# Reordering norms, moments and four copies in a three-layer attention kernel on one core

## The chip, the cores and the metric

The kernel runs on one core of a Trainium2 chip, as one program. The metric is the device time of an execution in microseconds (us), and the numbers given are medians over runs. A core has five engines that work side by side and meet at semaphores: TensorE (PE; its weight loads are listed apart as PEld), VectorE (DVE), ScalarE (ACT), GpSimd (POOL) and SyncE (SP), which here only issues DMA transfers. Each engine takes its own instructions strictly in the order in which the kernel writes them.

## The reference

Inputs are `x` and `ctx`, each 32 x 256 x 256 in fp32 (batch, tokens, features), and weights.

```python
# layer 0: attention with 16 heads of 16 columns; the result of batch element 0 is added to all 32
q, k, v = heads(x @ Wq.T), heads(ctx @ Wk.T), heads(ctx @ Wv.T)
x = x + attention(q, k, v, 1 / sqrt(16))[0]
# layer 1
norm_X = layernorm(ctx, n1w, n1b)
norm_F = layernorm(x, n2w, n2b)
attended = softmax(norm_F @ norm_X.T / 16) @ norm_X
h = gelu(attended @ fc1_w.T + fc1_b)                   # 4 hidden values per token
cross = h @ fc2_w.T + fc2_b
norm_cross = layernorm(cross, n3w, n3b)
self_att = softmax(norm_cross @ norm_cross.T / 16) @ norm_cross
out = norm_F + gamma2 * (cross + gamma1 * self_att)
```

In layer 0 only batch element 0 has to be computed. In layer 1 all 32 elements go through two layer norms, a 256 x 256 cross attention, and a self attention. Since `cross` has 4 hidden values and a bias behind it, the self attention needs few columns for each token (5 or 6 of a slot of 32).

## The kernel before

Everything of `x` stays in SBUF in one tile `x_all`, 128 partitions x 32 elements x 2 halves of the tokens x 256. Four batch elements make a quad; there are 8 quads. `ctx` comes in by quads into tiles `cq`, of which four exist at once. The order of the work on each engine is written out by hand (`tc.manual_schedule()`): the order of the calls is the order of the instructions on each engine's queue, and nothing is moved later. The one thing that the order does not settle is when a buffer is free: PSUM tiles come from pools with two banks for each of the tags `tp` and `et` (`bank`), and with two each for `sm` and `s` (pool `ps1`), and a tile waits for the readers of the tile that had its bank before.

The stages in order:

**Head, to about 53 us.** Layer 0 for element 0. `project(j)` and `head_step(j, ...)`, j = 0 to 3, each take four heads. `head_queries` (L392, L412) makes scores `sq` and VectorE takes their maxima `m_all`; `head_maxima` turns the maxima (`pm`) and adds them to the queries (`qmT`); `head_keys` (L437, L438) makes the scores `sk` again with the maxima taken off, and ScalarE exponentiates them into `eT_h`; `head_values` and `head_weighted` multiply by the values and divide (`ph`, `rd_h`, `att`). The three lists given to `head_step` put other work behind each of these: statistics and norms of the first three quads of `ctx`, the constants of the later layers, and the first transposes of `ctx` (`turn_c`). `turn_values` and `project_values` make the values `v1` of layer 0, in a bank `pp_v`.

**Steps 0 to 31, to about 190 us.** `first_step(s)` does the cross attention of one batch element s in a software pipeline. On each engine the calls of a step stand in the order of the function's text:

- `add_attention` has GpSimd issue a DMA that adds `att` to a quad of `x` (L647).
- `cross_turned(s - 2)` transposes the exponentials (TensorE, `pt_e`), and ScalarE copies them to `eTq` (L697).
- `stats_c(s + 12)` and `stats_x` let VectorE take means and variances of later elements (L202).
- `moments_x`, `moments_c` and `moments_both` turn those statistics into a factor `rs` and a shift `nmr`, on GpSimd (L213 to L227, with the power -1/2 in L218). They do so for 2, 4, 8 or 16 columns at once, one column for each half of an element; `moments_both(q + 2)` takes all of quad q + 2 of `x` and of quad q + 3 of `ctx`, 16 columns, in steps 7, 11, 15, 19.
- `turn_x(s + 1)` transposes the next element of `x` (`pt_x`), and ScalarE scales it into `nfT` (L657).
- `norm_x(n)` applies factor and shift to element n of `x`: half 0 on GpSimd (L298), half 1 on ScalarE (L300). From step 8 on n = s + 4.
- `turn_c(s + 4)` transposes an element of `ctx` (`pt_c`, TensorE), and VectorE copies it to `nxT` (L311).
- `norm_c(s + 8)` applies factor and shift to an element of `ctx`, both halves on GpSimd (L291, two instructions). Step s + 4 transposes it.
- `zeroed` clears tiles of the third layer in steps 8 to 15, and `scale_skip` (L666) scales `x` for the output from step 25 on; both are on GpSimd.
- `values`, `values_turned`, `cross_values` and `cross_weighted` (`pf`, `pv`) do the products with the values for a quad, in the second, third and fourth step of one.
- `cross_scores(s)` makes the scores `sc` (L675, TensorE), then VectorE takes the negated maxima `nm` (L685) and ScalarE the exponentials `e` (L688).
- Behind the step, at s = 3, GpSimd takes the moments of the fourth quad of `ctx` (`moments_c(3)`).

From step 20 the dictionaries `between` and `beside` add parts of the self attention to the steps: `hide` and `activate` (hidden values, GELU), `third_a` to `third_d` (layer norm and factors of the slots, GpSimd and VectorE; L854, L874 to L879, in which L876 is again a power), `turn_u`, `early_scores`, `early_weights`.

**Tail, to the end.** The steps B to B + 3 let the pipeline run empty. A loop over j = 3 to 7 works on the self attention by pairs of elements: `turn_t`, `turn_v`, `turn_u` transpose slots (L907 is the copy of `turn`), `pair_products` (L392) makes scores and outputs `po`, `scores_max` takes maxima, `weights` exponentials, `output` (L1040) adds to `x_all` and SyncE sends the result out. For j = 3, `turn_v(0)` is VectorE's, behind the maxima of the first pair.

Of the kernel before, what the change touches and what calls it, by code (L numbers as in the profile page):

```python
# [22 lines left out]
QB = 4  # L23
# [4 lines left out]
def tile_xattn_seq(  # L28
# [33 lines left out]
    nc = tc.nc  # L62
    B = x.shape[0]
# [16 lines left out]
    def bank(tag, name):  # L80
        return ps.tile([P, NC, D], F32, tag=tag, name=name)
# [178 lines left out]
    def moments_x(q, lo, hi):  # L260
        rn = moments(flat(st_of[q][:, 1, lo:hi]), (hi - lo) * NC, f"x{q}_{lo}")
        for b in range(lo, hi):
            mx_of[q * QB + b] = *rn, (b - lo) * NC
# [23 lines left out]
    def norm_c(n):  # L287
        rs, nmr, i = mc_of.pop(n)
        for t in range(NC):
            row = cq_of[n // QB][:, n % QB, t, :]  # L290
            nc.gpsimd.tensor_scalar(  # L291
                row, row, rs[:, i + t, :], nmr[:, i + t, :], ALU.mult, ALU.add
            )

    def norm_x(n):
        rs, nmr, i = mx_of.pop(n)
        row = x_all[:, n, 0, :]
        nc.gpsimd.tensor_scalar(row, row, rs[:, i, :], nmr[:, i, :], ALU.mult, ALU.add)  # L298
        row = x_all[:, n, 1, :]
        nc.scalar.activation(  # L300
            row, row, AF.Identity, bias=nmr[:, i + 1, :], scale=rs[:, i + 1, :]
        )
# [4 lines left out]
    def turn_c(n, copy=nc.vector.tensor_copy):  # L307
        q, b = n // QB, n % QB
        if b == 0:
            nxT_of[q] = wk.tile([P, QB, NC, D], F32, tag="nxT", name=f"nxT_{q}", bufs=2)  # L310
        copy(nxT_of[q][:, b], turned(cq_of[q][:, b], "tp", f"c_{n}"))  # L311
# [56 lines left out]
        nc.scalar.copy(wvT, turned(w_nat["v"], "tp", "wv"))  # L368

    def project_values():  # L370
        pp = bank("et", "pp_v")
        for t in range(NC):
            for dc in range(NC):
                nc.tensor.matmul(
                    pp[:, t, :],
                    c0T[:, dc, t * P : (t + 1) * P],
                    wvT[:, dc, :],
                    start=(dc == 0),
                    stop=(dc == NC - 1),
                )  # L380
        for t in range(NC):
            nc.vector.tensor_copy(
                v1[:, t, :, 0:DK], pp[:, t, :].rearrange("p (h e) -> p h e", e=DK)
            )
# [199 lines left out]
    def head_step(j, behind_queries=(), behind_maxima=(), behind_keys=()):  # L584
# [32 lines left out]
        2,  # L617
        [(head_values, 1), (project, 3)],
        [(head_weighted, 1), (setup_outer,), *((norm_c, n) for n in range(QB, 2 * QB))],
        [(turn_c, 0), *((stats_c, n) for n in range(2 * QB, 3 * QB)), (moments_c, 2)],  # L620
    )
    head_step(
        3,
# [7 lines left out]
        [(turn_c, 4)],  # L631
    )
    head_values(3)
    turn_c(5)
    head_weighted(3)


# [124 lines left out]
    def first_step(s, between=()):  # L762
        q, b = s // QB, s % QB
        if b == 0 and 2 <= q and q + 4 < NQ:
            load_c(q + 4)
        if s in (2, 3):
            add_attention((s + 1) * QB, (s + 2) * QB)
        elif b == 0 and 0 < q < NQ - 4:
            add_attention((q + 4) * QB, (q + 5) * QB)
        if 0 <= s - 2 < B:  # L770
            cross_turned(s - 2)
        if s < QB:
            stats_c(s + 3 * QB)
        if 2 <= s < 2 * QB:
            for n in (2 * s, 2 * s + 1):
                stats_x(n)
            if s < QB:
                ends = first_moments(2 * s, 2 * s + 2)
        if QB <= s and s + 3 * QB < B:
            stats_c(s + 3 * QB)  # L780
        if s >= 2 * QB and s + 2 * QB < B:
            stats_x(s + 2 * QB)
        if s == QB + 1:
            moments_x(2, 0, QB)
        if b == QB - 1 and 3 <= q + 2 < NQ:
            if q + 3 < NQ:
                moments_both(q + 2)
            else:
                moments_x(q + 2, 0, QB)
        if QB < s < B - 1:  # L790
            turn_x(s + 1)
        for n in {5: (8,), 6: (9, 10), 7: (11,)}.get(s, (s + QB,) if s > 7 else ()):
            if n < B:
                norm_x(n)
        if s + QB < B and s >= QB:
            turn_c(s + QB)
        if s >= QB and s + 2 * QB < B:
            norm_c(s + 2 * QB)
        for n, at in enumerate(scaled_at):
            if s == at:  # L800
                scale_skip(n)
        if 2 * QB <= s < 2 * QB + len(zeroed):
            nc.gpsimd.memset(*zeroed[s - 2 * QB])
        if b == 2 and 1 < q < NQ:
            values_turned(q)
        if b == 1 and 1 < q < NQ:
            values(q)
        if b == 2 and 0 < q <= NQ:
            cross_values(q - 1)
        if b == 3 and 0 < q <= NQ:  # L810
            cross_weighted(q - 1)
        for f, *args in between:
            f(*args)
        if s < B:
            softmax = cross_scores(s)
            if s <= QB:
                turn_x(s + 1)
            if s == 0:
                add_first(3)
            softmax()  # L820
        if s in (2, 3):
            ends()
        if s == QB - 1:
            moments_c(3)


    n_flat = n_all.rearrange("p g t b c -> p (g t b) c")
# [228 lines left out]
    for j in range(3, NQ):  # L1056


        turn_t(j - 1)
        sc0, b0 = pair_bank("s0", f"sc0_{2 * j}")  # L1060
        sc1, b1 = pair_bank("s1", f"sc1_{2 * j - 3}")
        pair_products(by_queries(2 * j, b0), by_keys(2 * j - 3, b1))
        if j == 3:
            first_step(B + 3)
            hide(6, 8)
            activate(6)
            third_a(3)
        scores_max(2 * j, sc0)
        turn_v(j - 3, by_vector if j == 3 else nc.scalar.copy)
        weights(2 * j - 3, sc1)  # L1070
        if j + 1 < NQ:
            turn_u(j + 1)
        po = out_banks(2 * j - 6)
        sc0, b0 = pair_bank("s0", f"sc0_{2 * j + 1}")
        pair_products(to_output(2 * j - 6, po), by_queries(2 * j + 1, b0))
        if j < NQ - 1:
            output(2 * j - 6, po)
            scores_max(2 * j + 1, sc0)
        else:
            scores_max(2 * j + 1, sc0)  # L1080
            output(2 * j - 6, po)
        self_values(j - 2)
        if j == NQ - 1:
            break
        if j == 3:
            third_b(3)
        if j == 4:
            third_d(3)
        sc1, b1 = pair_bank("s1", f"sc1_{2 * j - 2}")
        po = out_banks(2 * j - 5)  # L1090
        pair_products(by_keys(2 * j - 2, b1), to_output(2 * j - 5, po))
        weights(2 * j - 2, sc1)
        pa = self_weighted(j - 2)
        output(2 * j - 5, po)
        divide(j - 2, pa)
        if j == 3:
            third_c(3)
        done = len(scaled_at) + max(3 * (j - 3), 4 * (j - 3) - 2)
        for n in range(done, min(done + (3 if j < 5 else 4), B)):
            scale_skip(n)  # L1100
# [94 lines left out]
```

## Time and profile before

| what | value |
|---|---|
| median of 3 runs | 253.17 us |
| lowest and highest of the runs | 253.0 and 260.94 us |
| the profiled execution, time | 252.99 us |
| its span, first to last instruction | 251.0 us |
| its mean granted TensorE clock | 0.986 of full speed |
| TensorE busy | 219.1 us (87% of the span) |
| GpSimd busy | 181.7 us (72%) |
| VectorE busy | 171.7 us (68%) |
| ScalarE busy | 138.8 us (55%) |
| read from HBM, written to it | 17.73 MB, 8.39 MB |

The profile is of one execution. A row of a timeline gives the start in the span (us), the length, the engine, the line of the kernel, the operation with what it writes and reads, and in brackets how long the engine stood idle before it and what ended that. "x2" says that two such instructions ran one after the other. The chain of waits is followed back from the last instruction: at each step to what released it, or to the instruction before it on its engine. A name such as `pt_c` stands for all tiles of that name.

### The profile page before, as it was taken

Reading aid. Unit: us, or ns where it says so; the run is one execution under the profiler, and the core shown is the slowest. Engines: PE = TensorE matmul, PEld = TensorE weight load, DVE = VectorE, ACT = ScalarE, POOL = GpSimd, SP = SyncE. Lnnn points to the kernel's source line nnn. Section 1 sums busy time; section 2 is a strip of 40 time slices with the busy share of each in tenths; the row PEclk is TensorE's granted clock in tenths of the full one; section 3 lists DMA queues with packets and bytes.
Section 4 is the critical chain, followed back from the end, with each engine's and each line's share of the span. In section 5 each row is a group of like instructions: output and inputs, shape, how many; then the busy total and the mean of one; then the engine's idle time right before and its main releaser. Section 6 shows DMA issues by size and latency. Waiting matters only on the chain.

```text
span 251.0 us, 4961 instructions
## 1 busy us (share of the span) xinstructions
PE 219.1 (87%) x1813; PEld 159.5 (64%) x1813; DVE 171.7 (68%) x411; ACT 138.8 (55%) x271; POOL 181.7 (72%) x284
## 2 busy tenths in 40 slices
PE   8978785778975999999999997899999699999970
PEld 6656453446763979788797885666666455665540
DVE  1587875599897576778676684663546487876482
ACT  2231443447864976858768948538534735554610
POOL 8007999784799998999859999984159619999200
PEclk9999999999999999999999999999999889999996
DMA  6869999499999565390000000000000023442467
GB/s 210 292 192 373 387 387 330 169 203 251 208 183 158 167 106 107 125 168 2 3 1 1 3 0 3 0 5 2 3 0 0 3 111 142 167 161 93 171 228 275
DMA packets 18054, 33.81 MB, mean 135 GB/s; under 512 B 1191, under 2 KB 2158, under 8 KB 18030
## 3 DMA queue, kind: packets, MB, share of 16 engines
q1 hardware_dynamic: 13518, 25.37, 28.3%
q0 software_dynamic: 3696, 7.34, 16.9%
q10 hardware_dynamic: 816, 0.79, 0.9%
q8 instruction: 14, 0.23, 0.4%
q14 instruction: 10, 0.08, 0.1%
HBM read 17.73 MB, written 8.39 MB: 104 GB/s over the span
## 4 chain that ended last, share of the span: by engine, by line
PE 61%; DVE 19%; POOL 12%; ACT 3%; issue 3%; DVEq 0%; POOLq 0%; ACTq 0%
PE sc L675 16%; PE sc L392 9%; PE pt_c L193 4%; PE pt_x L193 4%; DVE st L202 4%; PE pt_e L193 3%; PE po L392 3%; PE pv L318 3%; PE pu L318 2%; POOL r L876 2%; PE pp L357 2%; POOL rs_x L218 2%; DVE x_all L1040 2%; PE pf L318 2%; DVE m_all L412 2%
## 5 line engine op out<-in xcount | busy, mean ns | idle before, releaser
L675 PE MATMUL sc<-nxT,nfT 128*128 128x256 f32 x256 | 62.5, 387 | 1.6 <-ACT nfT L657 1.6
L675 PEld LDWEIGHTS sc<-nxT,nfT 128*128 128x128 f32 x256 | 45.7, 190 | 13.3 <-issue 4.9
L688 ACT ACTIVATE e<-sc,nm 128x256 f32<-128x256 f32 x64 | 26.7, 470 | 25.8 <-DVE nm L685 25.8
L685 DVE TENSOR_REDUCE nm<-sc 128x2 f32<-128x512 f32 x32 | 22.1, 689 | 27.3 <-PE sc L675 14.1
L666 POOL TENSOR_TENSOR x_all<-x_all,w_bc 128x512 f32<-128x512 f32 x32 | 39.6, 1280 | 0.0
L657 ACT ACTIVATE nfT<-pt_x,bq,wq 128x256 f32<-128x256 f32 x64 | 33.1, 578 | 3.1 <-PE pt_x L193 3.1
L311 DVE COPY nxT<-pt_c 128x512 f32<-128x512 f32 x27 | 18.3, 679 | 11.2 <-PE pt_c L193 11.2
L193 PE MATMUL pt_x<-ident,x_all 128*128 128x128 f32 x132 | 20.3, 276 | 4.2 <-POOL x_all L298 1.9
L202 DVE BATCH_NORM_STATS2 st<-x_all 128x6 f32<-128x256 f32 x64 | 23.2, 412 | 0.1
L193 PE MATMUL pt_e<-ident,e 128*128 128x128 f32 x128 | 19.8, 276 | 2.2 <-ACT e L688 2.1
L392 PE MATMUL po<-w_out,vt 32*128 32x256 f32 x128 | 18.6, 417 | 3.4 <-DVE vt L907 2.2
L193 PE MATMUL pt_c<-ident,cq 128*128 128x128 f32 x132 | 20.3, 276 | 1.3 <-DVE ut L900 0.8
L1040 DVE TENSOR_TENSOR x_all<-po,x_all 128x512 f32<-128x512 f32 x26 | 16.7, 684 | 6.5 <-PE po L392 5.4
L202 DVE BATCH_NORM_STATS2 st<-cq 128x6 f32<-128x256 f32 x56 | 20.2, 412 | 0.0
L193 PEld LDWEIGHTS pt_x<-ident,x_all 128*128 128x128 f32 x132 | 15.5, 142 | 6.8 <-POOL x_all L298 3.3
L392 PE MATMUL sc<-ut 32*128 32x256 f32 x128 | 19.7, 419 | 0.0
L697 ACT COPY eTq<-pt_e 128x512 f32<-128x512 f32 x32 | 18.6, 585 | 1.9 <-PE pt_e L193 1.8
L291 POOL TENSOR_SCALAR cq<-cq,rs_b,nmr_b 128x256 f32<-128x256 f32 x32 | 19.4, 682 | 0.0
L392 PE MATMUL sc<-tt,ut 32*128 32x256 f32 x128 | 19.4, 403 | 0.0
L193 PEld LDWEIGHTS pt_e<-ident,e 128*128 128x128 f32 x128 | 15.4, 141 | 6.1 <-ACT e L688 3.2
L291 POOL TENSOR_SCALAR cq<-cq,rs_c,nmr_c 128x256 f32<-128x256 f32 x32 | 17.9, 589 | 0.1
L193 PEld LDWEIGHTS pt_c<-ident,cq 128*128 128x128 f32 x132 | 15.0, 141 | 4.0 <-issue 1.4
(204 smaller groups left out, 442.9 us busy)
## 6 DMA issues: line engine op xcount, KB each, us to landing
out_dram<-x_all SPq DMA_DIRECT2D x16, 512.0 KB
cq<-in_ctx_dram SPq DMA_DIRECT2D x7, 1024.0 KB
x_all<-att POOLq DMA_DIRECT2D x7, 1024.0 KB, 9.7
x_all<-in_x_dram SPq DMA_DIRECT2D x6, 1024.0 KB
x_all<-in_x_dram SPq DMA_DIRECT2D x1, 1792.0 KB
cq<-in_ctx_dram SPq DMA_DIRECT2D x1, 768.0 KB
wq_nat<-in_L_xattn_Wq_dram ACTq DMA_DIRECT2D x1, 256.0 KB
x_all<-in_x_dram SPq DMA_DIRECT2D x1, 256.0 KB
```

Source lines behind the costliest of these rows:

```text
L193: nc.tensor.transpose(pt[:, dc, t * P : (t + 1) * P], src[:, t, dc * P : (dc + 1) * P], ident)
L202: nc.vector.bn_stats(st[:, t, :], src[:, t, :])
L291: nc.gpsimd.tensor_scalar(row, row, rs[:, i + t, :], nmr[:, i + t, :], ALU.mult, ALU.add)
L311: copy(nxT_of[q][:, b], turned(cq_of[q][:, b], "tp", f"c_{n}"))
L392: nc.tensor.matmul(dst[i][:, t, :], lhs[r : r + SL, t * P : (t + 1) * P], rhs[r : r + SL, :], start=True, stop=True,)
L657: nc.scalar.activation(nfT_of[n][:, dc, :], px[:, dc, :], AF.Identity, bias=bq[:, dc : dc + 1], scale=wq2[:, dc : dc + 1],)
L666: nc.gpsimd.tensor_mul(x_all[:, n], x_all[:, n], w2_bc.unsqueeze(1).to_broadcast([P, NC, D]))
L675: nc.tensor.matmul(sc[:, qt, :], nfT[:, dc, qt * P : (qt + 1) * P], nxT[:, dc, :], start=(dc == 0), stop=(dc == NC - 1),)
L685: nc.vector.tensor_reduce(nm, sc, AX.X, ALU.max, negate=True)
L688: nc.scalar.activation(e[:, qt, :], sc[:, qt, :], AF.Exp, bias=nm[:, qt : qt + 1])
L697: nc.scalar.copy(eT_of[q][:, b], turned(e_of.pop(n), "et", f"e_{n}"))
L1040: nc.vector.tensor_add(x_all[:, n], po[i], x_all[:, n])
```

## The change

Six things change. (1) The bank of `pp_v` is taken from the tag `tp` instead of `et`. (2) The copies of `turn_c(0)` and `turn_c(5)` in the head go from VectorE to ScalarE. (3) The moments of x's third quad (elements 8 to 11) are taken in two pairs, at the end of steps 4 and 5, instead of all four at the start of step 5; x's norms 8 to 11 move to the ends of steps 5, 6, 6 and 7, behind those steps' exponentials on ScalarE; and the moments of the fourth quad of `ctx` move from the end of step 3 to the end of step 6. (4) c's norms, which ran eight elements ahead of the scores and four steps ahead of their transposes (steps 4 to 23), run six elements ahead of the scores and two steps ahead of their transposes: c 12 at the end of step 6, and element s + 6 in step s for s = 7 to 25. (5) x's norms of the last quad come one step later (s = 25 to 28, element s + 3). (6) In the tail `turn_v(0)` moves ahead of the first pair's products. No operation is added but one more set of moments (two of 4 columns in place of one of 8), and none is taken away.

```diff
--- before.py
+++ after.py
@@ -368,7 +368,7 @@
         nc.scalar.copy(wvT, turned(w_nat["v"], "tp", "wv"))
 
     def project_values():
-        pp = bank("et", "pp_v")
+        pp = bank("tp", "pp_v")
         for t in range(NC):
             for dc in range(NC):
                 nc.tensor.matmul(
@@ -617,7 +617,11 @@
         2,
         [(head_values, 1), (project, 3)],
         [(head_weighted, 1), (setup_outer,), *((norm_c, n) for n in range(QB, 2 * QB))],
-        [(turn_c, 0), *((stats_c, n) for n in range(2 * QB, 3 * QB)), (moments_c, 2)],
+        [
+            (turn_c, 0, on_scalar),
+            *((stats_c, n) for n in range(2 * QB, 3 * QB)),
+            (moments_c, 2),
+        ],
     )
     head_step(
         3,
@@ -631,7 +635,7 @@
         [(turn_c, 4)],
     )
     head_values(3)
-    turn_c(5)
+    turn_c(5, on_scalar)
     head_weighted(3)
 
 
@@ -780,8 +784,6 @@
             stats_c(s + 3 * QB)
         if s >= 2 * QB and s + 2 * QB < B:
             stats_x(s + 2 * QB)
-        if s == QB + 1:
-            moments_x(2, 0, QB)
         if b == QB - 1 and 3 <= q + 2 < NQ:
             if q + 3 < NQ:
                 moments_both(q + 2)
@@ -789,13 +791,14 @@
                 moments_x(q + 2, 0, QB)
         if QB < s < B - 1:
             turn_x(s + 1)
-        for n in {5: (8,), 6: (9, 10), 7: (11,)}.get(s, (s + QB,) if s > 7 else ()):
-            if n < B:
-                norm_x(n)
+        if 2 * QB <= s < B - 2 * QB:
+            norm_x(s + QB)
+        elif B - 2 * QB < s <= B - QB:
+            norm_x(s + QB - 1)
         if s + QB < B and s >= QB:
             turn_c(s + QB)
-        if s >= QB and s + 2 * QB < B:
-            norm_c(s + 2 * QB)
+        if QB + 2 < s < B - QB - 2:
+            norm_c(s + QB + 2)
         for n, at in enumerate(scaled_at):
             if s == at:
                 scale_skip(n)
@@ -820,8 +823,18 @@
             softmax()
         if s in (2, 3):
             ends()
-        if s == QB - 1:
+        elif s == QB:
+            moments_x(2, 0, 2)
+        elif s == QB + 1:
+            norm_x(2 * QB)
+            moments_x(2, 2, QB)
+        elif s == QB + 2:
+            norm_x(2 * QB + 1)
             moments_c(3)
+            norm_x(2 * QB + 2)
+            norm_c(3 * QB)
+        elif s == QB + 3:
+            norm_x(2 * QB + 3)
 
 
     n_flat = n_all.rearrange("p g t b c -> p (g t b) c")
@@ -1057,6 +1070,8 @@
 
 
         turn_t(j - 1)
+        if j == 3:
+            turn_v(0, by_vector)
         sc0, b0 = pair_bank("s0", f"sc0_{2 * j}")
         sc1, b1 = pair_bank("s1", f"sc1_{2 * j - 3}")
         pair_products(by_queries(2 * j, b0), by_keys(2 * j - 3, b1))
@@ -1066,7 +1081,8 @@
             activate(6)
             third_a(3)
         scores_max(2 * j, sc0)
-        turn_v(j - 3, by_vector if j == 3 else nc.scalar.copy)
+        if j > 3:
+            turn_v(j - 3)
         weights(2 * j - 3, sc1)
         if j + 1 < NQ:
             turn_u(j + 1)
```

## The prediction

> **What bounds the kernel now.** I read the page first, then the chain of waits in order of time, then timelines where that chain leaves TensorE.
>
> ```profile
> PE 219.1 (87%) x1813; PEld 159.5 (64%) x1813; DVE 171.7 (68%) x411; ACT 138.8 (55%) x271; POOL 181.7 (72%) x284
> ```
>
> TensorE is busy 87% of the span, so time is lost where it waits. GpSimd (POOL, 72%) is next. The chain in order of time (start, us, what):
>
> ```profile
> 70.73 1.65 POOL rs_c L218
> 72.87 1.34 POOL x_all L647
> 74.21 1.15 POOL cq L291 x2
> 76.49 1.66 POOL rs_x L218
> 80.38 1.08 POOL x_all L298 x2
> 81.48 0.63 PE pt_x L193 x4
> ...
> 97.74 1.73 PE sc L675 x8
> ...
> 103.39 0.44 PE pt_c L193 x4
> ```
>
> From 60 to 81 us the chain is mostly GpSimd's moments and norms; from 81 to 141 us it is TensorE. The scores of steps 4 to 13 start at 66.78, 71.90, 76.03, 82.60, 85.80, 89.84, 94.29, 97.74, 100.78 and 104.82. Where TensorE waits for nothing a step takes 3.04 (11 to 12), with pt_v 3.45 (10 to 11), with pv and pt_f 4.45 (9 to 10). Step 6 to 7 takes 6.57 and should take 3.45. ScalarE's timeline there says why:
>
> ```profile
> 78.66 0.60 ACT L300 ACTIVATE x_all<-x_all,nmr_x,rs_x 128x256 f32<-128x256 f32 x1 [4.86 <-POOL nmr_x L227]
> ```
>
> ScalarE stands 4.86 us at its half of x's norm 8; the exponentials of step 5 are queued behind it, and TensorE waits for them. The next views are GpSimd's at step 11, then all engines around step 25:
>
> ```profile
> 98.40 0.23 POOL L213 TENSOR_TENSOR df_b<-st 128x16 f32<-128x16 f32 x1 [0.98 <-DVE st L202]
> 99.69 2.93 POOL L218 TENSOR_TENSOR rs_b<-ve_b,neg_half 128x16 f32<-128x16 f32 x1
> 103.10 0.56 POOL L298 TENSOR_SCALAR x_all<-x_all,rs_b,nmr_b 128x256 f32<-128x256 f32 x1
> 103.64 1.09 POOL L291 TENSOR_SCALAR cq<-cq,rs_b,nmr_b 128x256 f32<-128x256 f32 x2
> ```
>
> ```profile
> 148.30 0.60 PE L193 MATMUL pt_c<-ident,cq 128*128 128x128 f32 x4
> 151.72 0.60 ACT L300 ACTIVATE x_all<-x_all,nmr_x,rs_x 128x256 f32<-128x256 f32 x1 [4.11 <-POOL nmr_x L227]
> 152.22 1.10 POOL L291 TENSOR_SCALAR cq<-cq,rs_b,nmr_b 128x256 f32<-128x256 f32 x2
> 199.41 0.86 PE L392 MATMUL po<-w_out,vt 32*128 32x256 f32 x2 [2.21 <-DVE vt L907]
> ```
>
> Once in four steps a block of moments over 16 columns holds GpSimd from 98.40 to 103.10, and the norms of that step come behind it. That costs nothing now: c's norm in that place is needed four steps later.
>
> **Part 1, ScalarE copies keys 0 and 5.** VectorE's rows in order:
>
> ```profile
> 33.74 0.69 DVE L311 COPY nxT<-pt_c 128x512 f32<-128x512 f32 x1 [1.27 <-PE pt_c L193]
> 34.35 2.70 DVE L202 BATCH_NORM_STATS2 st<-cq 128x6 f32<-128x256 f32 x8
> 36.97 2.40 DVE L412 TENSOR_REDUCE m_all<-sq 128x4 f32<-128x1024 f32 x3
> ```
>
> Without the copy the statistics start at 32.46 (end of mkT) and end at 35.2. The maxima then wait only for their scores (34.34 + 1.15), so they start at 35.5 and not at 36.97: 1.5 earlier, and pm, qmT, sk, eT_h, ph and att follow one another from there. Key 5's copy (46.49 to 47.18) stood before rd_h, whose input was there at 46.80: 0.2. ScalarE has room: 35.20 to 36.55 and 46.31 to 48.00 are free, a copy takes 0.59. GpSimd bounds the gain: its norms of c's third quad end at 46.99 and the DMA issue behind them takes 0.9, so rs_x cannot start before 47.9 (before: 49.90), at most 2.0 earlier. I take -1.6; bounds 0 and -2.0. If ScalarE had no room, the copy would push eT_h by its 0.59.
>
> **Part 2, pp_v in the other bank.** The last ten sq matmuls waited for the copies of v until 18.48 and may go 0.4 earlier. VectorE is busy without a gap from 17.58 to 22.07, which hides it: 0, bounds -0.4 and 0.
>
> **Part 3, order on GpSimd, steps 4 to 9,** on the clock of before. Norms of x 6 and 7 end at 69.54. DMA issue 0.89 (72.86 to 73.75): 70.43. Moments of 4 columns: 1.19 of small operations, pow 1.03, two products 0.50, so 2.72: 73.15. x 8 (0.55): 73.70. Second pair (its statistics end at 72.84): 76.42; x 9: 76.97. c's moments (69.54 to 72.86, 3.32): 80.29; x 10: 80.84; c 12 (1.08): 81.92; moments of 16 columns (4.7): 86.6; c 13: 87.7; x 11, DMA, x 12, c 14: 90.7. ScalarE's half of x 8 now stands behind the exponentials, so step 7's scores start at 76.03 + 3.45 = 79.5, 3.1 earlier; step 8's at 82.5 (x 9 and c 12 are in time, c 12 by 0.2). Step 9 wants c 13 at 82.5 + 1.73 + 0.87 = 85.1 and gets it at 87.7: TensorE waits 2.5 (its first transpose needs only half of c 13), and its scores start at 87.7 + 0.4 + 1.0 = 89.1 instead of 89.84. Net -0.75; bounds -3.1 (c 13 in time) and +0.5 (GpSimd's rows 1.2 longer). SP's load of c 6 waits for step 7's transposes only, so it comes earlier and delays nobody.
>
> **Part 4, c's norms two steps ahead.** From step 11 on, step s norms c s+6, which step s+2 transposes. The instruction order of the built program shows the 16-column moments of steps 11, 15 and 19 straight ahead of c 17, 21 and 25. In the fence above that place ends at 104.73, while TensorE wants c 17 at 103.39: 1.34 late, 1.2 after the first transpose. The same two rows are 119.73 against 118.37 and 134.69 against 133.36. The moments start when VectorE's statistics are done, and those follow the scores of the step before, so a stall moves both alike and the next quad pays again: 3 x 1.2 = +3.7; bounds 0 and +4.1. Behind the waiting transposes stand pf and sc, hence the whole step.
>
> **Part 5, steps 23 to 26.** x's last norms one step later take ScalarE's 4.11 us wait off the exponentials of step 24. But c 29 now sits where c 31 sat, behind pow of r (2.92), w_k and x's last moments: 152.22 to 153.3, with two of VectorE's rows out of its way 153.05, and TensorE wants it at 148.30. It stands 4.7, step 25's scores start at 154.4 instead of 149.83. Then sc 1.9, VectorE's nm and ut (1.4, they free pt_c's bank), pt_c, pt_f and pv (1.66): step 26 at 159.4 instead of 156.80, so +2.7; bounds -1.9 (c 29 in time) and +3.1. c 30 and c 31 follow in time.
>
> **Part 6, first output's v.** Its copy moves into idle VectorE time at 195. The pair behind po writes the bank that the maxima (197.81 + 1.22) read, so po and sc gain only 0.1: -0.1.
>
> **Clock.** At the tail the granted clock falls (columns: window, length, busy by engine, clock, DMA, GB/s):
>
> ```profile
> 200.00:201.00 1.00, 1.00 (x16) 0.88 (x10) 0.00 (x0) 0.99 (x2) 0.00 (x0) 0.50 0.00 0
> ```
>
> It is half from 199.5 to 202.8, right behind the 2.2 us in which TensorE stood. Price: sixteen po and sc matmuls took 2.1 (1.16 at 207.38), sixteen pu 1.70 (1.07), so 1.6, of which VectorE, busy from 201.51 on, passes on about 1.0. The gap of 1.65 us at 78 cost no clock. In the changed kernel the tail's gap shrinks to 1.4: -0.9. The 4.7 us of step 25 should cost +1.3, the 2.5 us of step 9 as likely as not, +0.5. Net +0.9; bounds -1.0 and +2.5.
>
> [...]
>
> **Sum.** -1.6 + 0 - 0.75 + 3.7 + 2.7 - 0.1 + 0.9 = +4.85. The profiled execution took 252.99 (span 251.0 and 1.99 around it): 257.8. The median of the runs is 253.17, 0.2 above it. About 2%, 248.1 to 258.2, is what a measurement of this kernel can tell from no change.
>
> **Rivals.** (A) GpSimd keeps up: c's norms arrive in time everywhere. Then 252.99 - 1.6 - 3.1 - 1.9 - 1.0 = 245.4, faster. For it: GpSimd had 0.98 us to spare at 98.4 and whole gaps near 124 and 197. Against it: c 17 sits behind 4.7 us of moments in a fixed order; it decides only if that block took under 3.4 us, and three rows of pow say 2.92 each.
> (B) Quads absorb their stalls, through later slack of 1.2 each: 257.8 - 3.7 = 254.1. For it: step 21 to 22 takes 4.58 where 4.45 would do, so a little slack exists; against it: the chain is TensorE without a break from 82 to 141.
> (C) The clock becomes the bound: head gain lost (+1.6) and both new gaps at half clock (+0.5 more): 259.9. For it: 2.2 us sufficed once; against: 1.65 did not, and part 1's rows are plain.
>
> **How the numbers follow.** Forecast 0.52, own range 256.3 to 259.2, about two fifths of it (0.21) above 258.2; A 0.10, since one mis-sized row of GpSimd decides three parts; B 0.19; C 0.19. Faster: A without its slow edge, 0.09. Slower: C and 0.21 of the forecast, 0.40. Same: the rest, 0.51. The range reaches from B to just past C, 253.8 to 260.2; left out are A and the outer edges.
>
> **What would show it.** Right: ScalarE's 4.86 and 4.11 us waits gone; TensorE waiting for POOL cq before pt_c in steps 9, 13, 17, 21 (about 1.2 in the last three) and 25 (about 4.7); statistics ahead of the fourth maxima ending near 35; clock 0.5 after step 25 and 1.0 at the first output. It would be wrong if pt_c waited for no cq, or if those waits were there and the scores of step 21 still started before 133.8 (134.79 before).

## The result, and the profile after

The changed kernel takes 262.55 us (median of 4 runs, 261.36 to 264.1). Against the kernel before the ratio is 1.038, with an interval of 1.028 to 1.047: 3.8% slower, where 257.8 and a range up to 260.2 had been predicted. The profiled execution took 262.4 us (span 260.6, clock 0.962); the one before had taken 252.99 (span 251.0, clock 0.986). The times of the kernel before go in step with its granted clock, from 252.5 at 0.985 to 261.2 at 0.946 in the runs made beside the experiments, so below single places are compared between profiled executions, by when the scores of a step start; the ratios leave out runs over 1.5% longer than the fastest of their kernel.

First the page of the changed kernel: busy time, the clock in 40 slices, the shares of the chain that ended last, and one of the costliest groups.

```profile
PE 224.6 (86%) x1813; PEld 161.3 (62%) x1813; DVE 171.5 (66%) x409; ACT 140.3 (54%) x273; POOL 183.3 (70%) x292
...
PEclk9999999999999799999999995999999979999995
...
PE 42%; POOL 34%; DVE 12%; issue 9%; DVEq 0%; ACT 0%; POOLq 0%; ACTq 0%
...
L193 PE MATMUL pt_c<-ident,cq 128*128 128x128 f32 x132 | 22.1, 285 | 11.0 <-POOL cq L291 9.4
```

The matmuls are the same 1813, yet TensorE is busy 224.6 us and not 219.1: some ran slower (the sixteen `pf` of step 9 took 1.93 us where others took 1.07). GpSimd's share of the chain went from 12% to 34%. The last line names the place: TensorE stands idle 11.0 us ahead of the transposes of `ctx`, 9.4 of it for c's norms (1.3 before, for another reason).

This table follows the scores (after less before, us, by their starts):

| scores of step | 0 | 6 | 7 | 8 | 9 | 10 | 12 | 13 | 17 | 21 | 24 | 25 | 26 | 31 | span |
|---|---|---|---|---|---|---|---|---|---|---|---|---|---|---|---|
| after less before | -1.30 | -1.31 | -4.52 | -3.95 | -0.71 | +0.03 | +0.03 | +1.55 | +3.07 | +4.60 | +4.47 | +10.55 | +9.81 | +9.88 | +9.6 |

So the change gains 4.5 us by step 7 and has lost it by step 10; then it loses 1.5 in steps 13, 17 and 21 each, and 6.1 at step 25.

**The gains.** VectorE in the head, then ScalarE in step 5 to 7, of the changed kernel:

```profile
32.48 2.70 DVE L202 BATCH_NORM_STATS2 st<-cq 128x6 f32<-128x256 f32 x8
35.61 2.42 DVE L412 TENSOR_REDUCE m_all<-sq 128x4 f32<-128x1024 f32 x3 [0.44 <-PE sq L392]
```

```profile
74.14 0.60 ACT L300 ACTIVATE x_all<-x_all,nmr_x,rs_x 128x256 f32<-128x256 f32 x1
74.63 0.58 ACT L701 COPY eTq<-pt_e 128x512 f32<-128x512 f32 x1
```

The fourth maxima start at 35.61 (36.97 before), and now wait for their scores, not for the statistics. ScalarE's half of x 8 stands at 74.14 without a wait (4.86 us before), behind the exponentials.

**The losses.** TensorE in step 9, then GpSimd and TensorE around step 13:

```profile
86.18 0.33 PE L193 MATMUL pt_c<-ident,cq 128*128 128x128 f32 x1 [1.72 <-POOL cq L291]
86.72 0.55 PE L193 MATMUL pt_c<-ident,cq 128*128 128x128 f32 x3 [0.22 <-POOL cq L291]
87.20 1.93 PE L318 MATMUL pf<-nxT,fc1T 128*32 128x256 f32 x16
89.06 2.73 PE L679 MATMUL sc<-nxT,nfT 128*128 128x256 f32 x8
```

```profile
98.43 0.23 POOL L213 TENSOR_TENSOR df_b<-st 128x16 f32<-128x16 f32 x1 [2.55 <-DVE st L202]
...
99.72 2.94 POOL L218 TENSOR_TENSOR rs_b<-ve_b,neg_half 128x16 f32<-128x16 f32 x1
...
103.67 1.10 POOL L291 TENSOR_SCALAR cq<-cq,rs_b,nmr_b 128x256 f32<-128x256 f32 x2
```

```profile
104.29 0.33 PE L193 MATMUL pt_c<-ident,cq 128*128 128x128 f32 x1 [0.87 <-POOL cq L291]
104.83 0.55 PE L193 MATMUL pt_c<-ident,cq 128*128 128x128 f32 x3 [0.21 <-POOL cq L291]
```

In both places c's norm (13, 17) stands behind a block of moments over 16 columns, as foretold. GpSimd stood idle 2.55 us ahead of the block at 98.43, for statistics of VectorE: it has time, but the order forbids the norm to use it. What the prediction gave only an even chance shows in the first fence: the sixteen `pf` take 1.93 us, the scores 2.73 (1.07 and 1.99 elsewhere). The clock had fallen to half (0.50 from 87.17 to 90.58) behind waits of 1.72 and 0.22 us. Next, all engines around step 25:

```profile
153.77 1.66 POOL L218 TENSOR_TENSOR rs_x<-ve_x,neg_half 128x8 f32<-128x8 f32 x1
...
156.52 2.18 POOL L291 TENSOR_SCALAR cq<-cq,rs_b,nmr_b 128x256 f32<-128x256 f32 x4
...
157.14 1.44 PE L193 MATMUL pt_c<-ident,cq 128*128 128x128 f32 x4 [4.20 <-POOL cq L291]
...
158.51 1.94 PE L318 MATMUL pf<-nxT,fc1T 128*32 128x256 f32 x16
...
160.38 2.91 PE L679 MATMUL sc<-nxT,nfT 128*128 128x256 f32 x8
```

TensorE stands 4.20 us (its weight loads another 0.36 within the 1.44) for c 29, behind r, `w_k` and x's last moments, and then runs at half the clock (0.50 from 155.44 to 162.26). In this trace the granted clock changes only at edges of a grid of 3.413 us, up to the closing outputs (71 windows from 5.25 to 247.60, each at 1.00 or 0.50); cut along that grid, the stretches of the changed kernel read (columns: window, length, busy by engine, clock, DMA share, GB/s):

```profile
83.76:87.17 3.41, 1.47 (x11) 0.91 (x9) 1.92 (x5) 1.70 (x5) 3.33 (x7) 1.00 0.04 15
87.17:90.58 3.41, 3.41 (x21) 1.85 (x21) 1.12 (x2) 1.65 (x4) 3.41 (x7) 0.50 0.50 86
152.02:155.44 3.42, 0.92 (x9) 0.68 (x7) 2.04 (x5) 2.18 (x6) 3.15 (x7) 1.00 0.00 0
155.44:158.85 3.41, 1.65 (x8) 0.89 (x12) 0.23 (x1) 0.73 (x2) 3.19 (x8) 0.50 0.00 0
158.85:162.26 3.41, 3.41 (x21) 1.91 (x14) 1.61 (x4) 0.00 (x0) 3.25 (x3) 0.50 0.00 0
```

The windows in which TensorE was busy 1.47, 0.92 and 1.65 us were each followed by one at half clock: one such at step 9, two at step 25. A fourth, from 210.05, lies in the tail behind a window of 1.90 us, where before had one too (from 199.45, behind 1.04 us).

### The profile page after: what moved, and what is told of

The parts are those of the page before. It is cut to its first block, busy times and chain, and to the rows that moved or that the text cites. A ratio compares the mean times of both kernels' runs of the same rounds, so it can differ in the third digit from the quotient of the medians.

```text
span 260.6 us, 4969 instructions
## 1 busy us (share of the span) xinstructions
PE 224.6 (86%) x1813; PEld 161.3 (62%) x1813; DVE 171.5 (66%) x409; ACT 140.3 (54%) x273; POOL 183.3 (70%) x292
## 4 chain that ended last, share of the span: by engine, by line
PE 42%; POOL 34%; DVE 12%; issue 9%; DVEq 0%; ACT 0%; POOLq 0%; ACTq 0%
PE sc L679 11%; PE sc L392 9%; POOL cq L291 7%; POOL rs_b L218 4%; PE pu L318 3%; PE pf L318 3%; PE pt_c L193 3%; PE pv L318 3%; POOL rs_x L218 3%; POOL rs_c L218 3%; PE po L392 2%; POOL r L889 2%; POOL x_all L298 2%; PE pt_e L193 2%; DVE st L202 2%
## 5 line engine op out<-in xcount | busy, mean ns | idle before, releaser
L679 PE MATMUL sc<-nxT,nfT 128*128 128x256 f32 x256 | 64.2, 394 | 1.6 <-ACT nfT L661 1.6
L679 PEld LDWEIGHTS sc<-nxT,nfT 128*128 128x128 f32 x256 | 46.8, 195 | 14.6 <-issue 5.7
L692 ACT ACTIVATE e<-sc,nm 128x256 f32<-128x256 f32 x64 | 26.8, 470 | 43.4 <-DVE nm L689 43.4
L193 PE MATMUL pt_c<-ident,cq 128*128 128x128 f32 x132 | 22.1, 285 | 11.0 <-POOL cq L291 9.4
L311 DVE COPY nxT<-pt_c 128x512 f32<-128x512 f32 x25 | 17.0, 680 | 13.1 <-PE pt_c L193 13.1
L392 PE MATMUL sc<-ut 32*128 32x256 f32 x128 | 18.8, 402 | 1.5 <-DVE t_sl L1031 1.5
L193 PE MATMUL pt_e<-ident,e 128*128 128x128 f32 x128 | 19.2, 274 | 0.0
L392 PE MATMUL po<-w_out,vt 32*128 32x256 f32 x128 | 18.0, 411 | 1.2 <-ACT vt L920 1.0
L291 POOL TENSOR_SCALAR cq<-cq,rs_c,nmr_c 128x256 f32<-128x256 f32 x32 | 18.6, 621 | 0.1
```

The source lines that it names most:

```text
L193: nc.tensor.transpose(pt[:, dc, t * P : (t + 1) * P], src[:, t, dc * P : (dc + 1) * P], ident)
L291: nc.gpsimd.tensor_scalar(row, row, rs[:, i + t, :], nmr[:, i + t, :], ALU.mult, ALU.add)
L392: nc.tensor.matmul(dst[i][:, t, :], lhs[r : r + SL, t * P : (t + 1) * P], rhs[r : r + SL, :], start=True, stop=True,)
L679: nc.tensor.matmul(sc[:, qt, :], nfT[:, dc, qt * P : (qt + 1) * P], nxT[:, dc, :], start=(dc == 0), stop=(dc == NC - 1),)
L692: nc.scalar.activation(e[:, qt, :], sc[:, qt, :], AF.Exp, bias=nm[:, qt : qt + 1])
```

## The experiments

Theory W, from the table: TensorE's waits for c 13, 17, 21, 25 and 29 are the loss, and the half clock behind the two long ones adds to it. Its rivals: a lead of two steps is too short wherever the norm stands; the moved x norms cost; the clock alone is the loss. "Lead" below is how much earlier a step's scores start than before.

### e4_filled: the clock by itself

```diff
+        for _ in range(times):
+            for i, (w, m) in enumerate(filler):
+                nc.tensor.matmul(pt[:, i, :], w, m, start=True, stop=True)
...
+    filled = {13: 2, 29: 5}
...
+        fill = [(ident, nxT_of[q - 1][:, 0, i, :]) for i in range(NC)] if n in filled else ()
```

> The changed kernel with matmuls that fill TensorE's waits at the two long places: ahead of the transposes of c 13 four matmuls of 128x256 (1.7 us) and ahead of those of c 29 ten (4.3 us) write the bank that the transposes then overwrite; they read ready data and their results are not used. Theory W with the clock apart: pt_c's starts stay where they are, the clock stays full in steps 9 and 25, the scores of step 10 start 1.6 earlier than the changed kernel's 94.25 and those of step 26 another 2.1 earlier: 258.5 to 259.5 against 262.4. Rival C0 (the slow matmuls behind the waits do not come from idleness): 262.4. Rival C1 (the clock is most of the loss and the waits would be caught up): under 256.

Measured: 259.9 (258.71 to 261.08), ratio to before 1.022 (1.008 to 1.036); the profiled execution took 259.37, the median is 0.4 above what was foreseen. TensorE in step 9 and step 25:

```profile
86.36 0.55 PE L196 MATMUL pt_c<-ident,cq 128*128 128x128 f32 x3 [0.21 <-POOL cq L294]
86.84 1.07 PE L327 MATMUL pf<-nxT,fc1T 128*32 128x256 f32 x16
...
155.71 0.55 PE L196 MATMUL pt_c<-ident,cq 128*128 128x128 f32 x3 [0.21 <-POOL cq L294]
156.19 1.07 PE L327 MATMUL pf<-nxT,fc1T 128*32 128x256 f32 x16
157.19 1.99 PE L688 MATMUL sc<-nxT,nfT 128*128 128x256 f32 x8
```

`pf` is back at 1.07. From step 7 to step 10 this kernel loses 2.95 (-4.88 to -1.93), the changed one 4.55: the clock's part is 1.60. From step 24 to 26 it loses 3.20 (2.51 to 5.71), the changed one 5.34: 2.14. Together 3.7 of the 9.4 us. The losses at c 17, 21 and 25 stay at 1.52 each, and the tail's window of half clock too. C0 and C1 fall.

### e3_near: the short lead by itself

```diff
-        if s >= QB and s + 2 * QB < B:
-            norm_c(s + 2 * QB)
+        if QB + 2 <= s < B - QB - 2:
+            norm_c(s + QB + 2)
```

> The kernel before with one thing changed: c's norms run two steps ahead of their transposes (element s + 6 in step s, from step 6), at their old place within a step. Theory W: the same waits as in the changed kernel at c 17, 21, 25 (1.5 each) and c 29 (about 5, with half clock behind it), a short one or none at c 13: 252.99 + 4.6 + 5.3 - 1 (GpSimd is freer in steps 4 to 6) = 261.5 to 263. Rival O (the new order in steps 4 to 9 is what makes GpSimd late everywhere): 253 to 254.

Measured: 267.42 (262.35 to 267.67); the run of 262.35, with a clock of 0.969, lies where it was foreseen, the other three have 0.942 or 0.943. The profiled execution (267.67) had four windows of half clock ahead of step 9 (three in the head, one at steps 7 and 8), where the profile before has none, so its scores of step 12 start 4.93 later. From there on it loses as the changed kernel does: 1.53, 1.53 and 1.52 in steps 13, 17 and 21, then 6.07 from step 24 to 25 (there 6.08). TensorE at steps 13 and 25:

```profile
109.19 0.33 PE L193 MATMUL pt_c<-ident,cq 128*128 128x128 f32 x1 [0.88 <-POOL cq L291]
109.73 0.55 PE L193 MATMUL pt_c<-ident,cq 128*128 128x128 f32 x3 [0.21 <-POOL cq L291]
...
162.04 1.44 PE L193 MATMUL pt_c<-ident,cq 128*128 128x128 f32 x4 [4.20 <-POOL cq L291]
```

The same waits to a hundredth, without any other part of the change. Rival O falls.

### e1_ahead: the same lead, another place

```diff
+        if s in (7, 11, 15, 19, 23):
+            norm_c(s + QB + 2)
         if b == QB - 1 and 3 <= q + 2 < NQ:
             ... moments_both(q + 2)
...
-        if QB + 2 < s < B - QB - 2:
+        if QB + 2 < s < B - QB - 2 and s not in (7, 11, 15, 19, 23):
             norm_c(s + QB + 2)
```

> The changed kernel with one order undone: in steps 7, 11, 15, 19 and 23 c's norm (13, 17, 21, 25, 29) stands ahead of that step's block of moments on GpSimd, not behind it; everything else, the two steps' lead too, stays. Theory W (the loss is TensorE's waits for these five norms, and the half clock that follows the two long ones): all five waits of pt_c for cq go, except some 0.6 at c 29, which still stands behind the third layer's power; the lead of 3.9 at step 8 is kept and step 26 adds some 1 to it: 248 to 249.5 against 252.99 before and 262.4 after. Rival D (a lead of two steps is itself too short, or x's moved norms cost): waits of over 1 us stay at the transposes and the time is above 257.

Measured: 251.9 (251.43 to 254.07), ratio 0.992 (0.978 to 1.006): 10.6 below the changed kernel, but not the 248 to 249.5 foreseen. Of the five waits 0.25 and 0.21 at c 29 are left; two others are there, at c 14 (shown) and, by 0.23 and 0.19, at c 18:

```profile
91.32 0.33 PE L193 MATMUL pt_c<-ident,cq 128*128 128x128 f32 x1 [0.60 <-POOL cq L291]
91.84 0.55 PE L193 MATMUL pt_c<-ident,cq 128*128 128x128 f32 x3 [0.19 <-POOL cq L291]
```

With a lead of two steps the block of moments now delays the norm of the step after. Step 10 loses 1.61 there and step 14 0.84; ahead of step 10 ScalarE also stands 2.81 for the factors of x 12, with exponentials behind it. From step 14 to 24, at the pace of before (0.16 to 0.25 later), c 22 and c 26 come in time. So rival D was right in part: with the norm ahead of the block, two steps keep the pace of before, but a TensorE that is ahead of it waits again.

### e2_far: four steps of lead again

```diff
-        if QB + 2 < s < B - QB - 2:
-            norm_c(s + QB + 2)
+        if s in (QB + 3, QB + 4):
+            norm_c(2 * s - 1)
+            norm_c(2 * s)
+        if QB + 4 < s and s + 2 * QB < B:
+            norm_c(s + 2 * QB)
```

> The changed kernel with c's norms four steps ahead of their transposes again from step 9 on (element s + 8 in step s; 13 and 14 in step 7, 15 and 16 in step 8), still behind the moments within a step. Theory W: the waits at c 17, 21, 25 and 29 are gone since the lead is back, the one at c 13 stays (about 1.9, with its half clock about as in the changed kernel): scores of step 10 near 94.2, as after, and those of step 24 near 145.7, as before; with x's last norms later step 26 is 2 earlier than before: 250 to 251.5; if the clock stays full at step 9, 248.5. Rival D (x's moved norms cost): above 257.

Measured: 253.0 (250.05 to 253.9), ratio 0.987 (0.956 to 1.019); the profiled execution, 250.05, lies in the range foreseen, the median does not. From step 10 to step 25 the lead stays at 0.36 to the hundredth: no wait at c 17, 21, 25, 29. The one at c 13 is there (1.68 and 0.21), this time without half clock behind it. Step 26 gives back 1.71, as foreseen.

### e5_only29: one norm

```diff
-        if QB + 2 < s < B - QB - 2:
+        if QB + 2 < s < B - QB - 2 and s != 23:
             norm_c(s + QB + 2)
+        if s == 21:
+            norm_c(29)
```

> The changed kernel with one instruction pair moved: c's norm 29 in step 21 instead of step 23, ahead of the third layer's power and of x's last moments. Theory W: the waits at c 13, 17 and 21 stay (scores of step 24 some 4.5 later than before), step 25 has no wait for cq and full clock, and step 26 gives back 1.7, since x's last norms no longer hold up the exponentials: scores of step 26 2.7 later than before, time 255 to 256 against 262.4. Rival C1 (what stalls there is taken up by other slack anyway): 260 or more.

Measured: 255.86 (254.58 to 257.74, 10 runs), ratio 0.999 (0.994 to 1.003). TensorE in step 25:

```profile
151.66 0.60 PE L193 MATMUL pt_c<-ident,cq 128*128 128x128 f32 x4
152.19 1.07 PE L318 MATMUL pf<-nxT,fc1T 128*32 128x256 f32 x16
```

No wait, full clock; step 25 adds 0.01, step 26 gives back 1.66. From step 24 to 26 it gains 1.65 where the changed kernel loses 5.34: moving two instructions of 0.55 us is worth 7.0 us there, and 6.7 in the medians. C1 falls.

### e6_best, e11_old_last_x, e12_old_turn_v: the good parts together, and two of them undone

e6_best, against the changed kernel:

```diff
+        if s == QB + 3:
+            norm_c(13)                     # ahead of moments_both
...
-        if 2 * QB <= s < B - 2 * QB:
+        if 2 * QB < s < B - 2 * QB:
             norm_x(s + QB)
...
-        if QB + 2 < s < B - QB - 2:
-            norm_c(s + QB + 2)
+        if QB + 4 < s and s + 2 * QB < B:
+            norm_c(s + 2 * QB)
+        if s == QB + 3:
+            norm_c(14)
+        if s == QB + 4:
+            norm_c(15)
+            norm_c(16)
...
+        elif s == 2 * QB:                  # behind the step's exponentials
+            norm_x(3 * QB)
```

> All that helped, together: the changed kernel with c's norms four steps ahead again from step 9 on, c 13 ahead of step 7's moments, c 14 behind them, c 15 and 16 in step 8, and x's norm 12 behind the exponentials of step 8. Theory W: no pt_c waits for cq over 0.5, the lead of 3.9 at step 8 (1.3 from the head, 2.6 from the order of steps 4 to 8) holds to step 25, step 26 adds 1.7: 247 to 249.5 by how many windows of half clock fall into the head; before 252.99 where it has one. Rival L (the lead is lost later to VectorE and GpSimd, as slack in the third layer's steps): 250.5 to 252.5.

Measured: 249.62 (248.19 to 250.84), ratio 0.978 (0.972 to 0.983): faster than both kernels. No `pt_c` waits for `cq`. But the lead of 4.33 at step 9 is 3.75 at step 11 and 2.44 from step 14 on; step 26 makes it 4.13, and 3.11 are left at step 31. Rival L has the course right, W the end. ScalarE at step 12 shows what stands ahead of the 1.31 lost at step 14:

```profile
102.19 0.60 ACT L300 ACTIVATE x_all<-x_all,nmr_b,rs_b 128x256 f32<-128x256 f32 x1 [3.41 <-POOL nmr_b L227]
102.70 0.82 ACT L692 ACTIVATE e<-sc,nm 128x256 f32<-128x256 f32 x2
```

This is the stall of x 8 once more, now at x 16: since TensorE is ahead, ScalarE reaches the norm before GpSimd has its factors, and the exponentials stand behind it. How much of the 1.31 is due to it, e13_quads asks.

e11_old_last_x, against e6_best:

```diff
-        elif B - 2 * QB < s <= B - QB:
-            norm_x(s + QB - 1)
+        elif B - 2 * QB <= s < B - QB:
+            norm_x(s + QB)
```

> The kernel of the run e6_best with x's last four norms back at their old places (element s + 4 in steps 24 to 27). Theory W: ScalarE stands some 4 us for the factors of x 28 in step 24 again, its exponentials and TensorE's step 26 behind it: step 25 to 26 takes 6.97 and not 5.26, scores of step 26 1.7 later than in e6_best: 249.5 to 252. Rival (VectorE's order in steps 25 and 26 sets that time): no change, 248 to 251.

Measured: 249.67 (248.59 to 250.79), ratio 0.989 (0.982 to 0.997).

```profile
149.51 0.60 ACT L300 ACTIVATE x_all<-x_all,nmr_x,rs_x 128x256 f32<-128x256 f32 x1 [4.10 <-POOL nmr_x L227]
```

ScalarE stands 4.10 again and step 25 to 26 takes 6.96: theory W. But of the 1.7 that e6_best gains there, 0.7 last, since steps 27 and 30 take back the rest (0.75 and 0.28); at step 31 the lead is 2.21 against 3.11, and 0.2 of that difference was there at step 25. Its median is that of e6_best within 0.1, so the runs don't tell the two apart.

e12_old_turn_v, against e6_best:

```diff
-        if j == 3:
-            turn_v(0, by_vector)
...
-        if j > 3:
-            turn_v(j - 3)
+        turn_v(j - 3, by_vector if j == 3 else nc.scalar.copy)
```

> The kernel of the run e6_best with turn_v(0) back behind the first pair's maxima. Theory W: the first output waits for vt again, TensorE stands some 2.2 us in one piece ahead of it instead of about 1.5, and more executions have half clock there: 0.1 to 1.5 longer than e6_best, 248.3 to 252. Rival (the place of turn_v carries the tail's time): over 2 longer.

Measured: 250.92 (249.62 to 253.64, 10 runs), ratio 0.990 (0.986 to 0.994). TensorE again stands 2.21 us in one piece for `vt`, and here two windows of half clock follow. From the scores of step 31 to the end the profiled executions took 62.3 in e6_best (no such window), 63.6 in the changed kernel (one), 63.8 before (one) and 65.4 here (two). With one window the old place took 63.6 to 64.1 (before, e9_head, e10_order), so against the changed kernel the place itself is worth 0.1 to 0.6; the rest is the clock.

### e13_quads: is it ScalarE's wait or GpSimd's pace?

```diff
-        if 2 * QB < s < B - 2 * QB:
+        if 2 * QB < s < B - 2 * QB and b > 0:
             norm_x(s + QB)
...
-        elif s == 2 * QB:
-            norm_x(3 * QB)
+        elif b == 0 and 2 * QB <= s < B - 2 * QB:
+            norm_x(s + QB)
```

> The kernel of the run e6_best with ScalarE's and GpSimd's norm of each quad's first x (16, 20; 12 was there already) moved behind the exponentials of its step, 12 and 16. Theory S (the 1.3 lost at step 14 in e6_best is ScalarE's 3.41 wait for the moments, with the exponentials behind it): scores of step 14 follow those of step 13 by 4.46 and not by 5.77, the lead of 3.75 holds to step 25 and the time is about 1 below e6_best: 247 to 250. Rival G (GpSimd's pace is the limit): the loss comes back at another wait within the next quad, 248.2 to 251 as e6_best.

Measured: 249.89 (248.18 to 250.45), ratio 0.978 (0.971 to 0.985). The condition holds for step 20 too, so x 24 moved as well. From step 13 to step 15 it loses 0.85 (-1.24 to -0.39) where e6_best lost 1.31: a third of the loss was ScalarE's wait at x 16. The rest comes back one norm later, where ScalarE stands for the same factors at x 17:

```profile
104.73 0.60 ACT L300 ACTIVATE x_all<-x_all,nmr_b,rs_b 128x256 f32<-128x256 f32 x1 [1.80 <-POOL nmr_b L227]
```

Step 22 loses 0.21 more, and the time is that of e6_best. That is rival G in the main: the factors come when GpSimd's block is through, and moving one norm moves the wait to the next. That GpSimd's pace is the limit from here on is argued from this, not tested by a faster block.

### e9_head, e10_order: parts of the change alone on the kernel before

e9_head:

```diff
-        pp = bank("et", "pp_v")
+        pp = bank("tp", "pp_v")
...
-        [(turn_c, 0), *((stats_c, n) for n in range(2 * QB, 3 * QB)), (moments_c, 2)],
+        [(turn_c, 0, on_scalar), *((stats_c, n) for n in range(2 * QB, 3 * QB)), (moments_c, 2)],
...
-    turn_c(5)
+    turn_c(5, on_scalar)
```

> The kernel before with the two edits of the head alone: ScalarE copies keys 0 and 5, pp_v takes the other bank. Theory W: the maxima of the fourth head step start some 1.4 earlier, the scores of step 0 start 1.3 earlier (up to half a us either way, by how the loads fall), and no later step gains or loses: 251.5 to 252 where the clock is as in the profile before. Rival (the copies only move VectorE's wait to ScalarE's exponentials): under 0.5 earlier, 253.

Measured: 254.28 (252.59 to 255.7, 10 runs), ratio 1.003 (0.996 to 1.009). The profiled execution had half clock from 26.8 to 30.2, so its scores of step 0 came 0.31 later than before and not 1.3 earlier. Behind that stretch the gain is there: the copy of `mkT` stands at 34.28, 1.99 later than before, so that the head gained 1.68 from there on. A gain of 1.7 at one place and a loss of 2.0 by a clock window at another: the time alone tells nothing here.

e10_order: of the edits of e6_best those in steps 4 to 8 and c's norms, without the head's, x's last norms and `turn_v`.

```diff
-        if s == QB + 1:
-            moments_x(2, 0, QB)
...
+        elif s == QB:
+            moments_x(2, 0, 2)
+        elif s == QB + 1:
+            norm_x(2 * QB)
+            moments_x(2, 2, QB)
...
```

> The kernel before with the order of steps 4 to 8 alone, as in the run e6_best (x's third quad in pairs, x 8 to 12 behind their steps' exponentials, c's fourth moments at the end of step 6, c 13 ahead of step 7's moments, c's norms four steps ahead from step 9). Head, x's last norms and turn_v as before. Theory W: ScalarE's 4.86 wait at x 8 is gone, step 7's scores start 3.2 earlier, step 8's 2.6, at most 0.6 of that is lost by step 10, and step 26 takes 6.97 as before: 250.5 to 251.5 where the clock is as in the profile before. Rival O (the step-7 gain needs the head's gain): under 1.5 at step 10.

Measured: 254.53 (252.28 to 257.78, 10 runs), ratio 1.002 (0.996 to 1.008). Step 7's scores start 3.30 earlier, as foreseen and without the head's part; but the lead is 2.49 at step 10, 2.15 at step 11 and 0.84 from step 14 on. Rival O falls by the steps; the expected time was missed, since the end of the lead at step 14 was not foreseen.

### e8_before_filled, e7_best_filled: the clock held up

```diff
+    def fill(dst, n):
+        for i in range(n):
+            nc.tensor.matmul(dst[:, i % 2 * P : (i % 2 + 1) * P], ident, ident)
```

> The kernel before with such fillers at five places: 5, 12 and 8 matmuls of 128x128 in the head, 14 ahead of step 7's transposes, 18 ahead of the first output pair. Theory P: every run at 251 to 253 with a mean clock over 0.98, where the kernel before spreads from 252.8 to 261.1 on one chip. Rival N: the spread stays.

Measured: 255.51 (254.48 to 255.8, 10 runs), ratio 1.000 (0.996 to 1.003). The page's clock in 40 slices:

```profile
PEclk9999999999999999999999999999999999999996
```

The spread is 1.3 us where the kernel before, beside it, went from 253.12 to 261.1; every run's clock lies between 0.988 and 0.992. The level is 1.5 above the 251 to 253 foreseen at its lowest: in the profiled execution the scores of step 0 start 1.67 later than before, and the lag stays. The tail, though it has no window of half clock now, is 0.72 longer too. So the fillers stand in the way of the chain. Theory P holds for the spread, not for the level.

> The kernel of the run e6_best with matmuls of 128x128 that fill TensorE's waits: 5 behind the second maxima of the head, 8 ahead of the fourth product with the values, 12 ahead of the first output pair; their results are not used. Theory P (the half clock follows a window of 3.413 us with too little matmul work in it, and the windows' place against the program differs from run to run): no half clock ahead of the closing outputs, every run at 246.5 to 248. Rival N (run-to-run differences come from elsewhere, or fillers delay the chain): the runs spread over 2 or more, or all are above 249.

Measured: 250.23 (249.61 to 251.31), ratio 0.979 (0.974 to 0.983); clock 0.986 to 0.991. No window of half clock ahead of the closing outputs, but all runs are above 249, as rival N has it for fillers that delay the chain: against e6_best's profiled execution the scores of step 0 start 0.46 later, and the stretch behind those of step 31 is 1.01 longer.

## Why the prediction was wrong, point by point

In the profiled executions the prediction's sum was +4.85, the measured one +9.41 (+9.62 in the span, -0.21 around it). Term by term, the clock's part taken from e4_filled:

| term | predicted | measured |
|---|---|---|
| part 1 and 2, head | -1.6 | -1.30 |
| part 3, steps 4 to 10, at full clock | -0.75 | -0.27 |
| part 4, c 17, 21, 25 | +3.7 | +4.57 |
| given back at step 22 | 0 | -0.13 |
| part 5, steps 25 and 26, at full clock | +2.7 | +3.20 |
| clock at steps 9 and 25 | +0.5 and +1.3 | +1.60 and +2.14 |
| tail: part 6 and its clock | -0.1 and -0.9 | -0.19 |
| around the span | 0 | -0.21 |

**Right.** The mechanism, its places and its signs. On the clock of before, c 17 was to end at 104.73 and ended at 104.74 (0.03 of shift aside); c 29 was to end at 153.05 and ended at 157.62, less the 4.47 of shift 153.15. ScalarE's two waits went (0.45 is left of the 4.11). The stalls repeated in each quad, so rival B fell; rival A fell. Rival C had the half clock behind both gaps right, but it let the gain of the head be lost, which was not, and its 259.9 was still too low.

**The step that failed most is "Clock."** Its two stalls were priced by the tail's 2.1 for 1.16 and by a chance of one half, and 0.9 was taken off for the tail. The runs show that a stall of 1.9 us can be followed by half clock (1.60; in e2_far, with 1.68 and 0.21, and in e5_only29, with 1.67 and 0.21, it was not), that one of 4.5 was followed by two windows (2.14), and that the tail, whose longest gap fell from 2.21 to 1.51, had a window of half clock all the same. That is 1.9 of the 4.6 us by which the sum was short, with 0.8 more in the tail. The reasoning from "1.65 cost no clock" was at fault: one execution shows where the grid happened to lie, not what a gap of that length does.

**Part 4 was 0.3 too small for each quad.** The prediction read from the chain of waits that TensorE wants c 17 at 103.39. In the timeline of before the group starts at 103.22: a row of the chain begins where the work before it ended, not where the instruction started. With that the norm is 1.51 late, and 1.52 is what each quad paid. So the 0.14 taken off, since the first transpose needs only half of the norm, was wrong too: the other three transposes, and the products behind them, wait for the second half whatever the first did.

**Parts 3 and 5** were 0.5 short each. The sums of GpSimd's rows came out within 0.3 (c 13 at 87.97 on the clock of before and not 87.7). In part 3 the gain by step 7 was 3.2 (3.1 foreseen), and from step 8 to 10 e4_filled lost 2.39, about as foreseen; what was put at nothing is step 8 itself, which came 3.61 behind step 7 and not 3.04. In the trace `pt_x` stands there until VectorE's copy `n_all` is done at 80.54; the rest of the 0.57 was not traced further. In part 5 TensorE's wait for the second half of the norm was again counted short (4.85 at step 25 in e4_filled, not 4.6), and step 26 gave back 1.65 and not 1.9; the prediction's own starts, 159.4 and 156.80, make 2.6 and not 2.7.

## What to carry to other kernels

Ahead of an instruction that another engine waits for, count what its own queue may hold at that moment, blocks that come once in several steps above all: where the lead ends before the block and what stands with it are done, the bottleneck engine stalls in every turn, here TensorE by 1.5 us each at c 17, 21 and 25. On the clock of before, c 17 ends 6.33 us after the start of the moments (98.40), and TensorE wants it after 4.82 (103.22): two steps of lead were not enough, since the moments start only when VectorE's statistics are done. On each engine's queue put what waits for slow factors behind what the bottleneck needs next; ScalarE's exponentials behind its half of a norm cost 3 us at x 8, and the same order at x 16 about 0.5 of the 1.31 lost there. Price waits of TensorE like those here (1.5 to 4.5 us) with a slow window that may follow (1.60 us at step 9, 2.14 at step 25), and compare such kernels step by step: the kernel before alone went from 252.5 to 261.2 us, in step with its granted clock, which is nearly the 9.4 of the change.

## What the runs showed of the hardware

**The granted clock changed on a grid of 3.413 us.** In all 15 profiled executions the changes of the granted clock ahead of the closing outputs lie on its edges (in the kernel before 71 windows from 4.89 to 247.23). The grid's place against the program differs from execution to execution: an edge lies at 4.89 us in the kernel before, at 5.25 in the changed one, at 2.89 in e9_head. Leaving out the last window ahead of the closing outputs' half clock in each, 1020 windows ran at full clock, and 19 of these were followed by half clock. TensorE was busy for 0.92 to 2.27 us in the 19; of the other 1001 none lies below 1.66, but 68 lie at 2.27 or below, so that from 1.66 to 2.27 busy time alone does not tell which is followed by half clock.

An estimate of the work from the timelines tells more. It counts each matmul at 0.217 us for 256 columns (eight scores took 1.73), weighted by the share of the 128 rows that it uses. By it the 19 held work for 0.18 to 0.39 of their window; of the other 1001 nine lie at 0.39 or below, the lowest at 0.36, so that only between 0.36 and 0.39 both occur. Without the weight the 19 go up to 1.34 (products on 32 rows run side by side: in the changed kernel `sc` from 209.06 and `po` from 209.07, 0.48 us for two of each) and the others down to 0.37, so that nothing separates them. By the weighted count the changed kernel's window from 206.64, with its products on 32 rows and 1.90 us busy, comes to about 0.3, and the one from 83.76, with its gap and 1.47 us, to about 0.25. The weighting is a fit to these windows; no run tests it by itself.

**So one gap may or may not cost.** The gap ahead of step 7 stood in the kernel before (first two lines) and in e9_head (last two), cut by the grid in two ways:

```profile
76.57:79.98 3.41, 1.76 (x8) 1.09 (x6) 2.85 (x8) 1.32 (x4) 3.22 (x6) 1.00 1.12 193
79.98:83.39 3.41, 2.48 (x18) 2.17 (x18) 1.60 (x5) 3.41 (x9) 3.32 (x9) 1.00 0.15 25
```

```profile
77.98:81.40 3.42, 1.23 (x6) 0.45 (x4) 2.59 (x7) 2.42 (x6) 3.23 (x8) 1.00 0.90 155
81.40:84.81 3.41, 3.01 (x13) 2.87 (x13) 0.86 (x3) 3.41 (x9) 3.16 (x9) 0.50 0.00 0
```

With 1.76 us of TensorE work in the window the clock stayed, with 1.23 it fell. The kernel before has gaps in the head (up to 1.8 us), at step 7 (1.65) and in the tail (2.21); in e8_before_filled, which fills them, the times lie between 254.48 and 255.8, where the kernel before went from 253.12 to 261.1. No long execution of the kernel before was profiled, so which of the gaps made its slow windows stays open.
